# Splitting one more output product into quarters, a shared tile for its block sums, and fewer quarter products where v or o stands alone

## The chip, the cores and the metric

The kernel runs on one core of a Trainium2 chip. The metric is the device time of one execution in microseconds (us); the time of a kernel is the median over runs. TensorE (PE) multiplies, VectorE (DVE) and ScalarE (ACT) work on its results in PSUM, GpSimd (POOL) works in SBUF only, and SyncE (SP) issues the DMAs. PSUM has eight banks, and this kernel hands them out one by one.

## The reference, cut to what matters

Two layers on x of 64 x 256 x 512 (float32). Layer 0 is a graph layer; layer 1 is attention over 8 heads whose scores are masked by the adjacency matrix. All matrices are float32.

```python
h = relu(layernorm(x));  x = x + (adj @ h) @ W0 + b0          # layer 0
h = relu(layernorm(x))                                        # layer 1
q, k, v = h @ Wq + bq, h @ Wk + bk, h @ Wv + bv               # 512 x 512 each
attn = softmax(q k^T / 8 + (1 - adj) * -1e9)                  # 8 heads of 64
x = x + (attn v) @ Wo + bo
```

## The kernel before, in words

**Groups and stages.** The batch of 64 is worked on in 32 groups of two (`GB = 2`, `NG = 32`). Layer 0 runs over all groups first, then layer 1. In layer 1 the program is a software pipeline: for group g the loop at L1365 onwards issues `attend(g, 0)`, `score(g, 1)`, then q and k of group g+1 (the **QK stage**), `attend(g, 1)`, `score(g+1, 0)`, then v of group g+1 together with the output product o of group g (the **VO stage**). `qd` 0 and 1 are the first and second four heads. From group 2 on (`FIRST2`) the four projections q, k, v and o use a two-level scheme; groups 0 and 1 use the one-level `project`. So there are 30 two-level QK stages (groups 2 to 31), and 28 two-level VO stages (o of groups 2 to 29). v of group 2 is worked out beside a one-level o, v of group 31 alone (order `V1` in both), o of group 30 alone (order `O1`) and o of group 31 alone at the very end (order `OL`).

**Products.** Each projection is a Strassen-Winograd product: seven half-size products called A to G (table `BLOCKS`), on sums of weight halves (s1 to s4) and of activation halves (t1 to t4). A half-size product at **full form** is four matmuls of 128 rows with 256 columns (`product` inside `quartered`). If its letter is in `SMALL`, it is split once more: seven matmuls with 128 columns on sums of quarters (the **quarter form**). The quarter sums of weights are made once (`block_sums`, tiles named spare), those of the activations for every group on POOL (`block_hidden`, `block_outputs`, class `Blocks`). In `SMALL`, q, k and v have B to G, and o has C, D, E and F.

**Steps.** `quartered` makes a table of small steps, named by projection, letter and step: `qDg` is step g of product D of q. A step is one matmul, or one DVE add, or one ACT copy. Four ways of putting a quarter product together matter here. `added` (C, D, E): matmuls a, c, d, g into a fresh PSUM tile, and adds b, e, f, h from it into the SBUF result; h is a DVE add of 128 x 256 and the last reader of the tile. Matmuls i, j, k go into the bank of the product sum. `staged` (F, G): matmuls a, c, d, f; ACT copies b, e, g into an SBUF tile; DVE adds h and l. `chain` (B): matmuls a, d, b, f; ACT copies c, e, g, n; one DVE add k. `put` and `more` move a product sum into the result (steps such as `kp110`, `km10`).

**Order.** Nothing is scheduled by a tool: the engines run the steps in the order of the strings `QK`, `VO`, `V1`, `O1`, `OL` (L214 to L243), read by `follow`. A bar ends a tick, at which due work from `after` is issued (POOL's sums for instance), and an x issues one exponential of the scores on ACT. Every engine takes its own instructions in this order.

**Banks.** `bank()` hands out the first fitting entry of a list of free banks, and `give()` puts a bank at the end of the list when the last step that uses its tile has been issued. The program then waits, by a semaphore, until that last use is really over. A matmul that opens a tile in a bank just given back thus waits for the last DVE or ACT reader of the tile before it.

**Tiles.** q and k of the first four heads have one SBUF tile each per batch entry (tags q00, q01, k00, k01). The block sums of o live in a kept tile (`KEPT["o"]`), part of what layer 0 left free.

Of the kernel before, what the change touches and what calls it, by code (L numbers as in the profile page):

```python
# [73 lines left out]
def general_path(tc, x, adj, w0, b0, wq, bq, wk, bk, wv, bv, wo, bo, out):  # L74
# [140 lines left out]
    "qFa kA0 qFb kA1 kFa qFc x qCa | kA2 kA3 kFb qGa kp000 qFd kFc | kp001 kFd qA0 qFe kFe qA1 x qFf kFf | qA2 "  # L215
    "qFg kFg qA3 qFh kFi kFh qp000 kFj kFk qp001 | qCi kFl qCj x kCa qCk qCb qFi kCb qFj qCl qGb qCc kp100 qCd | "
    "qFl kCc kp101 kCd kGa x qCe qGc kCe qGd kCf kGi qCf kGj | qGe kGk kGb qFk kCg qp100 qGf kCh kGc qp101 qCg "
    "kGd | qGg qCh kBa kGe kBb qGh qGi kBc qGj kGf qGl qDa kGg kBd | qBa qDb kBe qBb kGh kBn qGk qBc qDc kGl qDd "
    "kBf qDe qBd | qDf kBg kCi kCj qBn kCk qBe kBh kCl kBi qDg qBf | qDh qEa qBg kEa kBj qEb kDa kEb kBk qBh qBi "
    "kDb qBj kp110 | kEc qBk kp111 qEc qEd kDc qp110 km11 kDd qp111 kDi kEd kDe qEf | kDj kDf kEf kDk qm11 kEi "  # L220
    "qEe kEj kEe qDi qEf2 kEk km10 kDg kEl0 | qEi kEf2 qDj kDh qDk qEg kEl1 qEj qm10 qEk kEg qEl0 | kEl2 kEh qEh "
    "qEl1 qEl2 ")
VO = (
    "vA0 oAz vA1 oBz vA2 vA3 x | vFa vCi vCj vCk vFb vp00 vBa vBb vFc x | vFd vGa vCl vFi vFj vFe vFk vBc vCa vGb "
    "vFf | vCb vBd vFg vGc vGd vBe vCc vFh vGe vCd vFl x oA0 oEa | vCe vGf vCf vBf vp10 oEb oA1 vGg vCg vBn oA2 "
    "vGh vBg | oA3 vCh x vGl oB0 vBh op00 oFa vBi | oFb vBj vDa vBk vEa vGi vDb vEb vGj vp11 vGk vEc | vDc vm11 "
    "vEd vDd vEe vDi vEf vDe vDj vDf vDk vEi vEf2 vEj | vm10 vEk vDg vEl0 vEg vDh oFc oFd vEl1 oFi vEh oFe oFj | "
    "vEl2 oFk oDa oFf oCa oFg oB1 oCb oB2 oFh | oFl oEc oEd oCc op10 oCd oB3 oCe oCi | oCf oCj op11 oG0 oG1 oDb "
    "oEe oG2 oEf | oG3 oDc om11 oDd oCg oDi oDe oDj oDf | oDk oEi oCh oCk om10 oDg oEj oEk oDh oEg oCl0 | oEh "
    "oCl1 oEl ")  # L230
V1 = (
    "vFa vA0 vFb vA1 vFc vDa x vFd | vA2 vA3 vFe vBa vp00 vBb vFf | vGa vBc vFg vFi vFj vGb vFh x vFk vGc vFl vBd "
    "vGd | vCa vBe vGe vCb vp10 vBf vGf vCc vBn vDb vBg vCd vGi vGg vCe vGj | x vCf vGk vEa vGh vBh vGl vBi vEb "
    "vBj x vDc vBk vDd | vEc vDe vEd vDf vCg vp11 vCi vCh vCj vEf vCk vEe vm11 vDg | vDi vDj vEf2 vDk vDh vEi vCl "
    "vEj vEg vm10 vEk | vEl0 vEl1 vEh vEl2 ")
O1 = (
    "oEa oAz oA0 oBz oA1 x oB0 | oFa oCa oEb oFb oA2 x oA3 oDa oFc | oFd oB1 oFe x oB2 oFf oEc oEd oFg op00 | oB3 "
    "oFh oFi oCb oFj op11 oFk oCc x oCd oFl | oCi oDi op10 oCj oDj oDk oDb oCk oEe oG0 oEf oCl0 oDc | oEg oG1 "
    "oCl1 oEh oDd oG2 oCe oCf oG3 oDe | oDf oCg om11 oDg oCh oEi oDh oEj oEk om10 | oEl ")
OL = (  # L240
    "oAz oBz oA0 oA1 oCa oA2 | oA3 oFa oB0 oFb oB1 | oB2 op00 oDa oFc oCb oFd oB3 oFe oFi op11 oFf | oFj oFg oFk "
    "oCi oCj oFh oDi oFl oDj oDk oEa op10 | oDb oEb oG0 om10 oDc oDd oCk oDe oEc | oDf oEd oG1 oCl0 oG2 oEe oG3 "
    "oEf oCl1 oDg om11 oEg | oCc oCd oDh oEi oCe oEj oCf oEk oEh oCg oEl | oCh ")  # L243
# [3 lines left out]
def kernel(  # L247
# [331 lines left out]
    SMALL = {"q": "BCDEFG", "k": "BCDEFG", "v": "BCDEFG", "o": "CDEF"}  # L579
# [3 lines left out]
    def block_sums(n):  # L583

        todo = []
        for x in SMALL[n]:
            w = W[n][BLOCKS[x][0]]
            def part(i, j):
                return w[:, j, i * P:(i + 1) * P]
            s1, s2, s4 = (spare.pop(0) for _ in range(3))  # L590
            W2[n, x] = dict(a11=part(0, 0), a12=part(0, 1), a22=part(1, 1), s1=s1, s2=s2, s3=part(1, 0), s4=s4)
            eng = nc.vector if x in "BFG" and n in "qk" else nc.gpsimd
            for o, p, q, op in ((s1, part(1, 0), part(1, 1), ALU.add), (s2, s1, part(0, 0), ALU.subtract),
                                (part(1, 0), part(0, 0), part(1, 0), ALU.subtract), (s4, part(0, 1), s2, ALU.subtract)):
                todo.append((eng.tensor_tensor, o, p, q, op))
        return todo

    class Blocks:

        def __init__(self, x, t):  # L600
            self.x, self.t = x, t
# [4 lines left out]
        def operand(self, n):  # L606
            if n == "t3":
                n = "b12"
            if n[0] == "t":
                return self.t[..., {"t1": 0, "t2": 1, "t4": 2}[n], :]  # L610
            return self.x[..., int(n[1]) - 1, int(n[2]) - 1, :]
# [5 lines left out]
    def quartered(g, n, halves, blocks, by_token, place, first, seeds=None, multiplied=None, done=None):  # L617

        s, steps, banks, users, adds, mms = W[n], {}, {}, {}, {}, [0]

        def step(name, todo, *used, quadrant=None, mm=False):
            mms[0] += mm
            for b in used:
                users[b] = users.get(b, 0) + 1
            if quadrant is not None:
                adds[quadrant] = adds.get(quadrant, 0) + 1

            def run_it():
                todo()
                for b in used:  # L630
                    users[b] -= 1
                    if not users[b]:
                        give(banks.pop(b), b in ("pa", "pc"))
                if quadrant is not None:
                    adds[quadrant] -= 1
                    if done and not adds[quadrant]:
                        done(*quadrant)
                if mm:
                    mms[0] -= 1
                    if multiplied and not mms[0]:  # L640
                        multiplied()
            steps[n + name] = run_it
# [26 lines left out]
        def product(x, b, fresh):  # L669
            if fresh and seeds:  # L670
                step(f"{x}z", lambda: take(b, seed=seeds[b][:, None, :].to_broadcast([P, 2, N])), b)
            for i in range(4):
                def todo(i=i):
                    starts = fresh and not seeds and i == 0
# [46 lines left out]
        def chain(x, b):  # L721
# [14 lines left out]
            def add_rest():  # L736
                o = part(banks[b], 1, None)
                add(o, o, like(o, held[0]))
            copy("c", 0, 0)
            step(x + "n", keep_rest, t)  # L740
            copy("e", 1, 0)
            copy("g", None, 1)
            last_three(x, "hij", b)
            step(x + "k", add_rest, b)
# [42 lines left out]
        if "B" in SMALL[n]:  # L787
# [4 lines left out]
        for x, name, end, i in (("F", "p10", put, 0), ("G", "m11", more, 1)):  # L792
            if x in SMALL[n]:
# [4 lines left out]
        added("C", lambda: place(0, 0), quadrant=(0, 0))  # L798
        last_three("C", "ijk", "pb", dict(partial=True))

        def add_three(name, m, k):
            def todo():
                o, u = (t if first is None else t.rearrange("p m (h j) -> p (m h) j", j=P)
                        for t in (place(0, 0), banks["pb"]))
                add(o[:, m, 0:k], u[:, m, 0:k], o[:, m, 0:k])
            step(name, todo, "pb", quadrant=(0, 0))
        for name, m, k in (("Cl0", 0, N), ("Cl1", 1, P)) if first is None else (("Cl", slice(0, 3), P),):
            add_three(name, m, k)
        added("D", lambda: place(1, 0), quadrant=(1, 0))
        last_three("D", "ijk", "pc")  # L810
# [263 lines left out]
    KEPT = {}  # L1074

    def block_hidden(g, step):
# [3 lines left out]
        third = Blocks(x[:, 1, 0:2, :].rearrange("p c (n j) -> p c n j", j=P), KEPT["h3"][:, 3])  # L1080
# [6 lines left out]

    def block_outputs(g, step):
        x = OT[g][:, 2:4, :].rearrange("p c (k n j) -> p k c n j", k=GB, j=P)
        t = KEPT["o" if g < NG - 1 else "h3"]  # L1090
        both = Blocks(x, t[:, 0:2])
        last = Blocks(HO[g].all[:, 1:3].rearrange("p t c (n j) -> p t c n j", j=P), t[:, 2:4])
        if g == NG - 1:
            for part in (last.one(0), last.one(1), both):
                part.sums(nc.gpsimd)
        elif g == NG - 2:
            after(step, last.sums, nc.gpsimd)
            behind_seeds.append(lambda: both.sums(nc.gpsimd))
        else:
            after(step, last.sums, nc.gpsimd)  # L1100
            after(step, both.sums, nc.gpsimd)
        O2[g] = {"C": both.one(0), "E": both.one(1), "F": last.one(0), "D": last.one(1)}

    def queries_keys(g):

        for n, store in (("q", Q), ("k", K)):
# [5 lines left out]
            def place(i, k, n=n, store=store):  # L1112
                if (i, k) not in store[g]:
# [47 lines left out]
    def quartered_outputs(g):  # L1161
        halves, place, done = outputs(g)
        row = L1["o"][1]
        return quartered(g, "o", halves, O2.pop(g), True, place, None, {"pa": row[:, :HF], "pc": row[:, HF:]}, done=done)
# [50 lines left out]
    def attend(g, qd):  # L1215
# [65 lines left out]

        after(1, divide)
# [82 lines left out]
    for g in range(NG):  # L1365
# [9 lines left out]
        if g == 0:  # L1375
            for pool, n, tag, used in ((const, 4 * DC, "w0_sb", None), (const, 4, "w0_s1", None), (const, 4, "w0_s2", None),
# [3 lines left out]
                                       (act, 16, "yT1", ("o", 4))):  # L1380
# [5 lines left out]
                spare.extend(t[:, i, :] for i in range(first, n))  # L1386
        for n, at in (("q", 7), ("k", 16)) if g == 0 else (("v", 9),) if g == 1 else (("o", 9),) if g == 2 else ():
# [15 lines left out]
        if g + 1 < NG:  # L1403
# [18 lines left out]
            else:  # L1422
                steps = quartered(g + 1, n, halves, H2[g + 1], *rest, multiplied=multiplied)
                if FIRST2 <= g < NG - 2:
# [59 lines left out]
```

## Time and profile before

| what | value |
|---|---|
| median of 3 runs | 2599.08 us (2598.89 to 2599.2) |
| profiled execution | 2598.82 us |
| its span in the profile | 2597.0 us |
| PE busy | 2580.3 us, 99% |
| weight loads (PEld) busy | 2299.8 us, 89% |
| DVE busy | 1903.8 us, 73% |
| ACT busy | 1254.3 us, 48% |
| POOL busy | 1792.4 us, 69% |
| layer 0 (all groups), q and k of group 0 | 0 to about 638 us |
| one group of layer 1 in the steady part (score, QK, attend, score, VO, attend) | 61.36 us |
| stage with v of group 31 alone | 11.57 us |
| stage with o of group 30 alone | 13.21 us |
| stage with o of group 31, first matmul to the start of the last | 14.59 us |

An engine's busy time is the union of its instructions' times. In a timeline each line gives start and duration in us, then engine, source line, operation and tiles. A float32 matmul stands in the trace as two rows (x2), and so does its weight load. Since matmuls are pipelined, the pace of a run of matmuls is read from start to start, not from the durations. "Idle before" is the time for which the engine had nothing to run, followed by what ended it. The granted clock of PE was full (0.999 on average).

### The profile page before, as it was taken

What the parts mean: (1) busy time and instruction counts of PE and PEld (TensorE: products, weight loads), DVE (VectorE), ACT (ScalarE), POOL (GpSimd) and SP (SyncE); (2) the same over time, 40 slices, a digit from 0 to 9 for tenths busy, and PEclk for the clock granted to TensorE, in tenths of its full rate; (3) what the DMA queues carried; (4) which work ended last, traced back from release to release, by engine and by line L of the source; (5) the groups of instructions that cost most, each with busy time, mean ns of one, the idle gap of its engine ahead of it and who ended that gap; (6) DMA issues with size and microseconds to landing.
All of it is one profiled execution on the core that took longest, in us unless ns stands there. A gap on an engine that the chain in (4) does not pass through costs nothing.

```text
span 2597.0 us, 56864 instructions
## 1 busy us (share of the span) xinstructions
PE 2580.3 (99%) x21914; PEld 2299.8 (89%) x21914; DVE 1903.8 (73%) x4160; ACT 1254.3 (48%) x2942; POOL 1792.4 (69%) x2150
## 2 busy tenths in 40 slices
PE   9999999999999999999999999999999999999998
PEld 8999899988888888888888888888888888888887
DVE  6888888885467677777777777777777777777776
ACT  4545444443344445555555455544445445554543
POOL 6788887773686666666666666666666666666665
PEclk9999999999999999999999999999999999999999
DMA  5676666565111222211111111111112222111101
GB/s 149 195 193 184 170 168 182 159 159 134 33 50 50 65 63 64 57 50 50 50 50 50 50 50 50 50 50 50 50 50 62 62 60 65 50 50 50 50 34 50
DMA packets 281107, 211.36 MB, mean 81 GB/s; under 512 B 145920, under 2 KB 212992, under 8 KB 280832
## 3 DMA queue, kind: packets, MB, share of 16 engines
q1 hardware_dynamic: 280224, 206.89, 30.0%
q8 instruction: 175, 2.87, 0.5%
q10 hardware_dynamic: 608, 0.79, 0.1%
q14 instruction: 100, 0.82, 0.1%
HBM read 106.96 MB, written 100.66 MB: 80 GB/s over the span
## 4 chain that ended last, share of the span: by engine, by line


## 5 line engine op out<-in xcount | busy, mean ns | idle before, releaser
L1188 DVE SCALAR_TENSOR_TENSOR a<-sc,maskT 128x512 f32<-128x512 f32 x512 | 311.9, 681 | 259.9 <-PE sc L1181 255.7
L1246 POOL TENSOR_TENSOR as<-as 128x512 f32<-128x512 f32 x64 | 80.8, 1263 | 411.0 <-ACT as L1245 404.9
L1213 POOL TENSOR_TENSOR as<-a 128x512 f32<-128x512 f32 x256 | 318.7, 1279 | 29.9 <-ACT a L1206 24.7
L1206 ACT ACTIVATE a<-a 128x1024 f32<-128x1024 f32 x256 | 272.6, 1065 | 3.6 <-DVE a L1188 3.6
L1181 PE MATMUL sc<-q,k 64*128 64x256 f32 x2048 | 238.7, 383 | 0.0
L1181 PEld LDWEIGHTS sc<-q,k 64*128 64x128 f32 x2048 | 194.5, 187 | 44.8 <-issue 26.3
L1229 PE MATMUL pav<-a,v 128*32 128x256 f32 x4096 | 232.7, 379 | 0.0
L1229 PEld LDWEIGHTS pav<-a,v 128*32 128x32 f32 x4096 | 132.9, 110 | 88.2
L43 DVE BATCH_NORM_STATS2 st<-x 128x6 f32<-128x512 f32 x256 | 173.1, 676 | 9.2 <-DMA x<-in_x_dram 6.8
L1236 ACT ACTIVATE as<-pden 128x512 f32<-128x512 f32 x64 | 38.3, 599 | 287.2 <-PE pden L1222 286.3
L1020 ACT ACTIVATE h<-x,nb,rs 128x512 f32<-128x512 f32 x128 | 97.2, 807 | 97.4 <-POOL nb L55 85.9
L516 POOL TENSOR_TENSOR oT<-oT 128x512 f32<-128x512 f32 x31 | 39.4, 1271 | 149.4 <-DVE oT L1267 149.4
L891 ACT ACTIVATE h<-x,nb,rs 128x512 f32<-128x512 f32 x124 | 90.8, 803 | 52.1 <-POOL nb L55 47.2
L703 ACT COPY q_F<-q_Fs 128x128 f32<-128x128 f32 (+1 forms) x90 | 27.1, 301 | 157.6 <-PE q_Fs L666 157.6
L1110 ACT ACTIVATE q<-q_pa,bq_c 128x256 f32<-128x256 f32 (+1 forms) x150 | 61.5, 451 | 62.0 <-PE q_pa L666 49.7
L954 POOL TENSOR_TENSOR hs<-h 128x512 f32<-128x512 f32 x31 | 39.5, 1273 | 72.9 <-ACT h L891 72.9
L1026 DVE STREAM_TRANSPOSE r<-h 128x512 f32<-128x512 f32 x128 | 83.9, 689 | 7.2 <-ACT h L1020 6.8
L615 POOL TENSOR_TENSOR spare<-h1T,spare 128x128 f32<-128x128 f32 x180 | 82.5, 459 | 7.1
L839 DVE TENSOR_TENSOR x<-o_pa,x 128x512 f32<-128x512 f32 (+1 forms) x121 | 82.4, 681 | 6.0 <-PE o_pa L680 4.9
L516 POOL TENSOR_TENSOR t_y<-yT,t_y 128x512 f32<-128x512 f32 (+1 forms) x65 | 82.7, 1272 | 2.9 <-ACT yT L926 0.5
L1248 POOL TENSOR_TENSOR as<-as 128x512 f32<-128x512 f32 x64 | 80.8, 1262 | 5.3
L516 POOL TENSOR_TENSOR t_h<-h1T,t_h 128x512 f32<-128x512 f32 x64 | 81.9, 1280 | 2.5
(1633 smaller groups left out, 8587.2 us busy)
## 6 DMA issues: line engine op xcount, KB each, us to landing
residual<-x SPq DMA_DIRECT2D x256, 128.0 KB, 2.5
hidden<-r SPq DMA_DIRECT2D x128, 256.0 KB, 4.4
h1T<-hidden SPq DMA_DIRECT2D x64, 512.0 KB, 7.3
x<-residual SPq DMA_DIRECT2D x32, 1024.0 KB, 8.2
x<-in_x_dram SPq DMA_DIRECT2D x254, 128.0 KB, 3.0
out_dram<-x SPq DMA_DIRECT2D x62, 512.0 KB, 4.2
w_sb<-in_L_gnn_weight_dram SPq DMA_DIRECT2D x1, 1024.0 KB, 8.9
wq_sb<-in_L_gnn_Wq_dram SPq DMA_DIRECT2D x1, 1024.0 KB, 6.8
```

Of the source, the lines that this page charges most:

```text
L43: nc.vector.bn_stats(st, src)
L516: eng.tensor_tensor(self.t[n][:, c, :], self.operand(p, c), self.operand(q, c), op=ALU.subtract)
L615: eng.tensor_tensor(self.operand(o), self.operand(p), self.operand(q), op=ALU.subtract)
L839: nc.vector.tensor_tensor(o, ps, u, op=ALU.add)
L891: nc.scalar.activation(H0[g][:, t, :], xt[:, t, :], AF.Relu, bias=nb[:, t % n:t % n + 1], scale=rs[:, t % n:t % n + 1])
L1020: nc.scalar.activation(h1[:, k * NT + t, :], xt[:, k * NT + t, :], AF.Relu, bias=nb[:, t:t + 1], scale=rs[:, t:t + 1])
L1026: nc.vector.transpose(r[:, :, k, t, :], h1[:, k * NT + t, :].rearrange("p (j b) -> p j b", b=32))
L1181: nc.tensor.matmul(ps[j][:, kt * N:(kt + 1) * N], k[j * HD:(j + 1) * HD, c, kt * P:(kt + 1) * P], q[j * HD:(j + 1) * HD, c, :], start=(kt ...
L1188: nc.vector.scalar_tensor_tensor(o.rearrange("p k n -> p (k n)"), ps[j], SCALE, maskT_f, op0=ALU.mult, op1=ALU.add)
L1206: nc.scalar.activation(a, a, AF.Exp)
L1213: nc.gpsimd.tensor_tensor(AS[c, b], a4[:, :, 0, :], a4[:, :, 1, :], op=ALU.add)
L1229: nc.tensor.matmul(po[f][h * 32:(h + 1) * 32, b * N:(b + 1) * N], v[:, k, h * HD + f * 32:h * HD + f * 32 + 32], A[h // 2, b][:, (h % 2) * ...
```

## The change

1. **o's G at quarter form.** `SMALL["o"]` gets G. `staged` then makes product G of o out of seven matmuls of 128 columns, three ACT copies and two DVE adds, in place of four matmuls of 256 columns. Its four activation sums (`head_outputs`) are made on POOL behind the score matmuls of the next group.
2. **One tile for q's and k's first head pairs and o's block sums.** The four tiles of tags q00, q01, k00, k01 become one tile of tag qk0; o's block sums take the same tag, in turn with it. The third sums (t3) of B, and of o's G, get a place of their own, so that the unsplit operand stays whole.
3. **Fewer quarter products where v or o stands alone.** v of group 2 and of group 31 has B at full form. o of groups 30 and 31 has only E and F at quarter form: C and D become four 256-column matmuls each (G was at full form there and stays).
4. **`chain` puts B together differently.** A copy of 128 x 128, one of 128 x 256 and one add of 128 x 256 go; one copy of 128 x 128 and two adds of 128 x 128 come.
5. **All five orders are new.** In the bank list pb is now given back as fully written where C is at full form.

```diff
-    SMALL = {"q": "BCDEFG", "k": "BCDEFG", "v": "BCDEFG", "o": "CDEF"}
+    SMALL = {"q": "BCDEFG", "k": "BCDEFG", "v": "BCDEFG", "o": "CDEFG"}
+    BOTH = {"v": "B", "o": "CDG"}
...
+            s3 = spare.pop(0) if x in BOTH.get(n, "") else part(1, 0)
+            W2[n, x] = dict(a11=part(0, 0), a12=part(0, 1), a22=part(1, 1), s1=s1, s2=s2, s3=s3, s4=s4)
...
-            def add_rest():
-                o = part(banks[b], 1, None)
-                add(o, o, like(o, held[0]))
+            def with_rest(name, k):
+                step(x + name, lambda: add(part(banks[b], 1, k), total(), held[0]), t, b)
             copy("c", 0, 0)
             step(x + "n", keep_rest, t)
-            copy("e", 1, 0)
-            copy("g", None, 1)
+            with_rest("e", 0)
+            copy("g", 0, 1)
+            with_rest("k", 1)
             last_three(x, "hij", b)
-            step(x + "k", add_rest, b)
...
+        if "C" in small:
+            added("C", lambda: place(0, 0), quadrant=(0, 0))
...
+        else:
+            product("C", "pb", True)
+            more("m00", "pb", 0, 0)
+        if "D" in small:
+            added("D", lambda: place(1, 0), quadrant=(1, 0))
+            last_three("D", "ijk", "pc")
+        else:
+            product("D", "pc", False)
...
+    def head_outputs(g):
+        O2["t"] = t = act.tile([P, 16, P], F32, tag="qk0", name=f"to_{g}")
+        head = Blocks(HO[g].all[:, 0].rearrange("p c (n j) -> p c n j", j=P), t[:, 12:15], t[:, 15])
+        head.sums(nc.gpsimd)
+        O2[g] = {"G": head}
...
-                if (i, k) not in store[g]:
+                if (i, k) not in store[g] and not i:
+                    if g not in QK0:
+                        QK0[g] = act.tile([P, 2, GB, 2, N], F32, tag="qk0", name=f"qk_{g}")
+                    store[g][i, k] = QK0[g][:, "qk".index(n), k]
...
+        if qd and FIRST2 <= g < NG - 2:
+            behind_scores.append(lambda: head_outputs(g))
         after(1, divide)
```

The part of the order `QK` around the handing over of a bank from D of q to D of k, before and after (PE steps are those ending in a, c, d, g of D and E; a, b, d, f, h, i, j of B; a, c, d, f, i, j, k of G):

```diff
-    ... kCl kBi qDg qBf | qDh qEa qBg kEa kBj qEb kDa kEb kBk qBh qBi kDb qBj kp110 | ...
+    ... | qDf kBj qBf kp110 qGc qBk qDg kp111 qGd qDh kDa qBg qEc qGe km11 | qEd qBh qEf qBi kDb ...
```

## The prediction

> **What bounds the kernel now.** I first read the page's busy shares, then the list of what PE waited for, then the busy time by stage, and last single timelines. The page's chain of waits is empty for this run, so the bound has to come from these.
>
> ```profile
> PE 2580.3 (99%) x21914; PEld 2299.8 (89%) x21914; DVE 1903.8 (73%) x4160; ACT 1254.3 (48%) x2942; POOL 1792.4 (69%) x2150
> ```
>
> ```profile
> PE w_27a L523 <- DVE x L839: 1.2, 1, 1.2
> ...
> PE o_pa L680 <- DVE x L839: 0.7, 1, 0.7
> ```
>
> ```profile
> 1464.35:1486.76 22.41, 22.41 (x186) 21.88 (x184) 17.52 (x43) 15.56 (x44) 11.88 (x18) 1.00 0.26 69
> ...
> 1494.87:1517.61 22.74, 22.74 (x175) 21.79 (x173) 18.98 (x45) 10.68 (x26) 18.39 (x19) 1.00 0.01 1
> ```
>
> The second block lists PE's waits (total, times, longest): all are one or two events each, in layer 0 or at the end, under 10 us in all. The third gives, for one QK and one VO stage, length, then busy time of PE, weight loads, DVE, ACT and POOL. PE fills both stages wholly, at full clock. So in 28 VO and 30 QK stages a matmul that goes is time that goes, and a wait put before a matmul is time that comes; no engine behind PE can give it back.
>
> **The pace of matmuls.** One VO stage runs product G of o at full form, then small matmuls:
>
> ```profile
> 1513.11 1.89 PE L680 MATMUL o_pa<-wo_s,t_o 128*128 128x256 f32 x8
> 1514.83 0.39 PE L666 MATMUL o_Ds<-spare,spare 128*128 128x128 f32 x2
> ...
> 1516.39 0.39 PE L666 MATMUL o_pb<-wo_sb,spare 128*128 128x128 f32 x2
> ```
>
> Four 256-column matmuls (x8) go from 1513.11 to 1514.83, 1.72 us; the next seven 128-column ones start from 1514.83 to 1516.17 and the eighth at 1516.39, so seven take 1.56 us, 0.223 each.
>
> **Part 1, G of o at quarter form.** Per VO stage 1.72 goes and 1.56 comes: -0.16 us, and x 28 = **-4.5 us**. The Trainium skill speaks against such a split: Perfetto Trace Analysis, section Matmuls, says that larger matmuls are more efficient when possible. The row agrees only in that a column costs 4% more (2 x 0.223 against 0.43); by a rule of no splitting I would book a loss, by the row seven small ones still beat four large ones. I take the row.
> What comes with it: three ACT copies (0.27, 0.27, 0.37 by the rows of v's G), two DVE adds (0.42 and 0.70 by v's), four POOL sums of 128 x 256 (0.73 each, 2.9 us). DVE goes from 18.98 to about 20.2 of 22.6 us, the change of `chain` for v included (two 0.28 for one 0.43); ACT and POOL stay below. PE hides all three as long as no matmul waits for a late one. DVE may end the stage later by the 1.25 us added: it then has nothing until the next scores (idle 4.00 before its mask operation at 1523.29), which covers it.
>
> **Part 2, the shared tile.** The new POOL sums must wait until the score matmuls have read q and k; these end at 1494.87. POOL is then idle until DVE's oT at 1498.60 (4.97 us idle), and the 2.9 us fit in with 0.8 left. Were that cover gone, o's other sums and the key sums would queue behind; the key sums end at about 1513.4, and PE wants them at 1517.61, so that 4 us of slip would still cost nothing. In the other direction, the first write of q and k into the tile comes in the next QK stage, and PE's last use of o's sums lies an attend and a score stage (4.45 and 3.65 us) earlier. Cost: nothing. The DMA queues get no instruction more or less; only in the last group one write of the result stands earlier on SP's queue, which is empty there. The extra weight sums (four on POOL, 0.46 each, once) lie in group 2's QK stage, where POOL works 11.9 of 22.4 us: nothing.
>
> **Part 3, v and o alone.** B of v at full form: +0.16 in each of two stages. But these stages have a stall that its chain causes:
>
> ```profile
> 762.64 0.39 PE L666 MATMUL v_Cs<-wv_sb,h1T 128*128 128x128 f32 x2
> 762.67 0.25 ACT L729 COPY v_pc<-v_Bs 128x128 f32<-128x128 f32 x1
> ...
> 762.97 0.30 PEld L666 LDWEIGHTS v_Bs<-spare,spare 128*128 128x128 f32 x2
> 762.97 0.49 PE L666 MATMUL v_Bs<-spare,spare 128*128 128x128 f32 x2
> 763.00 0.59 ACT L1124 COPY v<-v_pa 128x512 f32<-128x512 f32 x1
> ...
> 763.19 0.30 PEld L666 LDWEIGHTS v_Gs<-spare,spare 128*128 128x128 f32 x2
> ```
>
> The pair at 762.97 was due at 762.86 (0.22 after 762.64) and waits for the copy that ends at 762.92: 0.11 late, and its row is 0.49 rather than 0.39 long, 0.10 more, because its weights are loaded only after the wait. With two smaller ones beside it about 0.3 goes: net -0.14 each, **-0.3 us**.
> o alone: C and D cost 2 x 0.16 more in each of two stages, +0.64. These stages wait for DVE's answers: o of group 30 takes 13.21 us against a pace of 11.40 (28 small matmuls at 0.223, 12 large at 0.43), o of group 31 takes 14.59 to the start of its last matmul against 11.18. DVE works 11.58 us of the first. C and D at full form take about 2 us of adds out of each stage (by their rows two of 0.28 and two of 0.42 for each letter; C's sum of 0.70 gives way to one add of 0.69; neighbours overlap by 0.08). The pace after is 20 x 0.43 + 14 x 0.223 = 11.72, and 0.10 is lost at the entry of every stage. Bounds: all other stalls gone, -1.4 and -3.0; none gone, +0.3 each. With that much less on the engine they wait for I take most: -0.9 and -2.3, **-3.2 us**. The tail behind the last matmul keeps its form (adds of 128 x 256 from its bank, then the write): nothing.
>
> **Part 4, chain.** For q and k one ACT copy goes and a larger one shrinks; DVE swaps 0.43 for two 0.28. In QK DVE works 17.5 of 22.4 us: nothing.
>
> **Part 5, the new orders.** This decides. Each fresh PSUM tile takes a bank whose last reader must be done. I went through QK and VO in both programs' order, and counted the matmuls between the last one into the old tile and the first one into the new tile of the same bank. In the order before it is never under five matmuls (1.12 us), nor after, with one exception: D of k takes the bank of D of q, as before, but `kDa` now stands directly behind `qDh`, and only `qGd` lies between `qDg` and `kDa`. All other banks are in use there, so no other can be had, and in the built program that matmul does wait for DVE. How long the answer takes stands in the trace of before:
>
> ```profile
> 1479.97 0.39 PE L666 MATMUL q_Ds<-spare,spare 128*128 128x128 f32 x2
> ...
> 1480.39 0.42 DVE L839 TENSOR_TENSOR q<-q_Ds,q 128x256 f32<-128x256 f32 x1
> ...
> 1481.09 0.39 PE L666 MATMUL k_Ds<-t_h,wk_sb 128*128 128x128 f32 x2
> ```
>
> `qDg` starts at 1479.97, its add `qDh` 0.42 later and takes 0.42; release to matmul is 0.05 (762.92 to 762.97). Sum 0.89. Before, `kDa` came 1.12 after `qDg`, so 0.23 to spare. After, it is due 2 x 0.223 = 0.45 after it: 0.44 late. To this comes the restart. The Trainium skill (TensorE: Matmul & The Clock Gate, Step-by-step: what each phase is for) says that PE's queue pulls weight loads ahead of running matmuls; by that the weights would be in place and the stall 0.44, x 30 = 13.2 us. The rows at 762.97 show weight load and matmul starting together after the release, and the pair 0.10 longer; with it 0.54, x 30 = **+16.3 us**. I take the row. DVE is free then: the add before, `qBk`, starts 0.42 after its matmul `qBf` and ends at 0.70, while `qDg` comes two matmuls after `qBf` and its add is due at 0.87. Queued behind `kDa` on PE are the 29 last matmuls of the stage and all later stages; nothing on PE can pass it.
>
> **Sum** on the profiled execution: 2598.82 - 4.5 - 0.3 - 3.2 + 16.3 = **2607.1 us**; this execution lies 0.26 under the median of the runs, so I say 2607.3, +0.3%.
>
> **Rivals.**
> 1. *The bank wait does not show* (the answer comes in time, or another wait in QK already covers it). Then 2598.8 - 8.0 = 2590.8, -0.3%. For it: PE has not one wait in the QK stages now, and an order this regular elsewhere. Against: 0.89 against 0.45, from rows of the same three steps. 0.07.
> 2. *The stall is there without the restart*, or the o stages gain all: 2598.8 - 4.5 - 0.3 - 4.4 + 13.2 = 2602.8, within 0.2% of before. For it: the skill's rule. Against: each stalled pair above. 0.12.
> 3. *A second wait in QK.* The steps after `kDa` stand closer to their answers than before (`kDg` behind `kDf`, `kEg` behind the adds of E, `qDg` behind `qDf`), with DVE at 80%. One more wait of 0.05 with a restart of 0.10 in each of 30 stages is +4.5: 2611.6; two give 2616. For it: new, dense order; against: the wait at `kDa` itself gives DVE 0.5 us to catch up. 0.23.
> The forecast itself has 0.58.
>
> **How the numbers follow.** Cases of a slower kernel hold 0.81. What a measurement tells from no change is 0.2%, 5.2 us: from 2593.9 to 2604.3 counts as the same. The forecast's own spread is the o stages (+-1.5) and the stall (0.49 to 0.60, 14.7 to 18): 2604.5 to 2610, with a sliver below the bound. Slower 0.80, same 0.13, faster 0.07. For 8 in 10 the range takes in rival 2 in its upper half and one more wait of rival 3: 2602.5 to 2613.
>
> **What would show it.** Right: in each QK stage one wait of PE on a k_Ds matmul, ended by a DVE add from q_Ds, about 0.4 long with a pair of 0.49; QK stage 22.95 rather than 22.41, VO 22.58 rather than 22.74; the stage of o 30 near 12.3. Wrong: QK still at 22.4 (rival 1), QK at 22.85 (rival 2), waits in QK on other tiles (rival 3), or VO longer than 22.74, which would mean that DVE at 90% or POOL's late sums hold PE up.

## The result, and the profile after

The changed kernel takes **2615.94 us** (median of 6 runs, 2615.07 to 2616.59), the kernel before 2599.3 us beside it: 1.0064 times as long, 95% interval 1.0051 to 1.0077. That is +16.6 us where +8.2 was forecast, and above the forecast range, which ended at 2613. The profiled execution has a span of 2614.6 us against 2597.0.

The list of PE's waits, which had nothing in it from the QK stages, now begins with one (what waited, for whom, total us, times, longest):

```profile
PE k_Ds L671 <- DVE q L850: 8.8, 30, 0.3
```

Three stages of the changed kernel, a QK stage, the score stage ahead of a VO stage, and that of VO (columns as before: stretch, length, busy time of PE, weight loads, DVE, ACT, POOL, then granted clock, DMA share and GB/s):

```profile
1535.43:1558.55 23.12, 22.83 (x187) 22.03 (x185) 18.07 (x44) 15.62 (x42) 11.89 (x18) 1.00 0.24 65
1563.00:1566.77 3.77, 3.72 (x36) 3.03 (x32) 2.54 (x5) 0.60 (x1) 2.24 (x3) 1.00 0.02 4
1504.75:1527.32 22.57, 22.57 (x178) 21.83 (x179) 19.42 (x48) 11.13 (x27) 20.08 (x23) 1.00 0.00 1
```

QK was 22.41 and is 23.12, with a PE that is no longer busy throughout; VO was 22.74 and is 22.57; the score stage was 3.65 and is 3.77. Taken from the first matmul of a stage to the first of the next, over the whole execution:

| stages | before, each | after, each | difference in all |
|---|---|---|---|
| 30 QK | 22.41 | 23.13 | +21.6 |
| scores ahead of VO | 3.65 | 3.77 (28 of 33) | +3.4 |
| one score stage ahead of QK, longer before | 3.99 | 3.65 | -0.3 |
| 28 VO | 22.735 | 22.572 | -4.6 |
| v of group 2 beside a one-level o, and v of group 31 alone | 23.68, 11.56 | 23.55, 11.46 | -0.2 |
| o of 30, o of 31 | 13.21, 15.08 | 12.46, 13.15 | -2.7 |
| behind the last matmul | | | -0.8 |

Layer 0 is 1.1 us longer in this one execution (607.29 to 608.43), with the same instructions; it varies from run to run by this much (607.28 and 609.08 in two of the experiments) and is not the change's.

The wait that the forecast named, in one QK stage of the changed kernel (start, duration, engine, line, tiles; idle time before and who ended it):

```profile
2481.31 0.39 PE L671 MATMUL q_Ds<-spare,spare 128*128 128x128 f32 x2
2481.53 0.39 PE L671 MATMUL q_Gs<-t_h,wq_s 128*128 128x128 f32 x2
...
2481.74 0.42 DVE L850 TENSOR_TENSOR q<-q_Ds,q 128x256 f32<-128x256 f32 x1
...
2482.22 0.49 PE L671 MATMUL k_Ds<-t_h,wk_sb 128*128 128x128 f32 x2 [0.29 <-DVE q L850]
```

`kDa` was due at 2481.76 (0.45 after 2481.31) and comes at 2482.22, 0.06 behind the end of the add: 0.46 late. (The bracket says 0.29 because the row before it runs on until 2481.92.) Its pair of rows is 0.49 long and not 0.39, and the next one is that 0.10 later. In the mean over the stages 0.456 and 0.101, in sum 0.557; thirty times that is 16.7.

Later in the same stage stands a second wait, which the list of waits does not show, since a wait shorter than the overlap of the rows leaves no idle time:

```profile
2484.49 0.42 DVE L850 TENSOR_TENSOR q_G<-q_Gs,q_G 128x256 f32<-128x256 f32 x1 [0.34 <-ACT q_G L708]
...
2487.14 0.75 DVE L850 TENSOR_TENSOR k<-k_Ds,k 128x128 f32<-128x128 f32 x2
...
2487.68 0.39 PE L671 MATMUL q_pa<-spare,wq_s 128*128 128x128 f32 x2
2487.95 0.49 PE L671 MATMUL k_Ds<-spare,spare 128*128 128x128 f32 x2
```

The last line is `kDg`. It was due at 2487.90 and comes at 2487.95, and the row of 0.49 gives it away. It adds to rows of the tile that DVE must have read before (`kDe`, `kDf`, the two adds to 2487.89). Those adds end a row of DVE work, with pauses of 0.10 at most, that began with `q_G`, and `q_G` had waited for ACT. The wait and the longer row cost 0.15 in each stage, 4.5 in all.

The third is at the start of VO, here in the changed kernel:

```profile
1564.83 1.89 PE L1207 MATMUL sc<-qk 64*128 64x256 f32 x16
...
1566.15 0.60 ACT L309 ACTIVATE o_pa<-bo_r 128x512 f32<-128x512 f32 x1 [4.22 <-DVE a L1214]
1566.77 0.51 PEld L685 LDWEIGHTS v_pa<-wv_sb,h1T 128*128 128x128 f32 x3 [0.45 <-DVE a L1214]
1566.77 0.70 PE L685 MATMUL v_pa<-wv_sb,h1T 128*128 128x256 f32 x2
```

In the kernel before, the seed came behind the first matmul of VO, which started at 1494.87:

```profile
1494.97 0.60 ACT L309 ACTIVATE o_pa<-bo_r 128x512 f32<-128x512 f32 x1 [4.82 <-DVE a L1188]
```

VO now begins with `oAz vA0` where it began with `vA0 oAz`. ACT's seed for o thus gets the first bank that DVE's masking of the scores frees, and v's first matmul the next one, freed by a later mask operation: 0.12 us of PE, in 28 stages. (The second experiment below tests this.)

### The profile page after: what moved, and what is told of

The parts are those of the page before. It is cut to its first block, busy times and chain, and to the rows that moved or that the text cites. A ratio compares the mean times of both kernels' runs of the same rounds, so it can differ in the third digit from the quotient of the medians.

```text
span 2614.6 us, 57520 instructions
## 1 busy us (share of the span) xinstructions
PE 2589.6 (99%) x22046; PEld 2306.5 (88%) x22046; DVE 1957.1 (75%) x4284; ACT 1277.4 (49%) x2930; POOL 1837.0 (70%) x2262
## 4 chain that ended last, share of the span: by engine, by line
PE 87%; DVE 5%; POOL 3%; DMA 2%; issue 1%; ACT 1%; SPq 1%; DVEq 0%; POOLq 0%; ACTq 0%
PE pav L1255 8%; PE sc L1207 6%; DVE a L1214 3%; PE pden L1248 2%; PE q_pa L671 2%; PE k_pa L671 2%; PE v_pa L671 2%; PE v_pa L685 2%; PE o_pa L671 2%; PE o_pc L685 2%; PE o_pa L685 2%; PE q_pa L685 2%; PE k_pa L685 2%; PE q_pc L671 2%; PE k_pc L671 2%; PE k_Ds L671 2%
## 5 line engine op out<-in xcount | busy, mean ns | idle before, releaser
L1207 PE MATMUL sc<-qk 64*128 64x256 f32 x1024 | 119.2, 382 | 0.0
L1207 PE MATMUL sc<-q,k 64*128 64x256 f32 x1024 | 119.2, 382 | 0.0
L1207 PEld LDWEIGHTS sc<-q,k 64*128 64x128 f32 x1024 | 97.1, 187 | 22.4 <-issue 13.2
L1207 PEld LDWEIGHTS sc<-qk 64*128 64x128 f32 x1024 | 97.1, 187 | 22.3 <-issue 13.1
L708 ACT COPY k_F<-k_Fs 128x128 f32<-128x128 f32 (+1 forms) x90 | 27.2, 303 | 157.2 <-PE k_Fs L671 157.2
```

Of the source, the lines that this page charges most:

```text
L1207: nc.tensor.matmul(ps[j][:, kt * N:(kt + 1) * N], k[j * HD:(j + 1) * HD, c, kt * P:(kt + 1) * P], q[j * HD:(j + 1) * HD, c, :], start=(kt ...
```

## Experiments

A kernel called "three moves" below has all of the first three edits; the "fastest" is the one with `kEf2` earlier. Times are medians. The runs fall into batches on several chips, and the kernel before took 2598.4 to 2599.5 in them, so a difference between batches is uncertain by about 1 us; where that matters, the stages of the profiled executions are given as well. The last column is the mean of the 30 QK stages.

| what runs | expected | measured | QK stage |
|---|---|---|---|
| `kDa` later | 2599.2 | 2609.10 | 22.92 |
| VO begins with `vA0` | 2612.5 | 2613.17 | 23.12 |
| `kDg` later | 2611.5 | 2614.63 | 23.09 |
| three moves | 2591.3 | 2604.97 | 22.88 |
| three moves, DVE shifted by 3 | 2594.9 | 2594.22 | 22.544 |
| three moves, DVE shifted by 1 | 2594.2 | 2594.63 | 22.542 |
| `kDa` later, DVE shifted by 3 | 2599.0 | 2598.89 | 22.58 |
| three moves, `kEf2` earlier | 2591.2 | **2591.48** | 22.44 |
| before, `kDa` earlier | 2616 | 2601.47 | 22.52 |
| fastest, G of o at full size, shifted | 2596.0 | 2601.32 | 22.43 |
| fastest, G of o at full size | 2603 to 2606 | 2601.89 | 22.43 |
| fastest, part 3 undone for o | 2594.9 | 2594.87 | 22.44 |

### The three waits one by one

`kDa` alone moved:

```diff
-    ... kp111 qGd qDh kDa qBg qEc qGe km11 | qEd qBh qEf qBi kDb ...
+    ... kp111 qGd qDh qBg qEc qGe km11 | qEd qBh qEf kDa qBi kDb ...
```

> The changed kernel with one token of QK moved: kDa stands five matmuls behind qDg (about 1.1 us) instead of one. Theory (each wait is priced by itself: 0.456 late + 0.101 restart in each of 30 QK stages): -30 x 0.557 = -16.7, so about 2599.2 us, no wait on k_Ds behind q's add of D; the small wait at kDg (0.05 + 0.10) stays, since DVE is idle for 0.34 us ahead of the chain of adds that kDg waits for; QK stage about 22.56. Rival A: the order as a whole is too dense for DVE, and the wait at kDa only shows where it first catches PE; with it gone DVE has 0.56 us less to catch up in each stage and the wait reappears at kDg (up to 0.6 there): gain under 5, about 2611 to 2615, QK stage near 23.0. Rival B: the stall is not this wait: no change, 2616.

Measured 2609.10: only 6.8 of the 16.7 came. `kDa` waits no more, but `kDg` now waits for longer than it did, 0.39 (934.32 to 934.71 below) against 0.05:

```profile
PE k_Ds L671 <- DVE k L850: 6.8, 29, 0.3
```

By time and by QK stage this lies between the theory and rival A. But rival A had a busy DVE in mind, and DVE was not busy (same view as above, the kernel with `kDa` moved):

```profile
930.90 0.42 DVE L850 TENSOR_TENSOR q_G<-q_Gs,q_G 128x256 f32<-128x256 f32 x1 [0.58 <-ACT q_G L708]
931.36 0.70 DVE L850 TENSOR_TENSOR q_pa<-q_pa,q_G 128x512 f32<-128x512 f32 x1
932.52 0.69 DVE L850 TENSOR_TENSOR q<-q_pa,q 128x512 f32<-128x512 f32 x1 [0.46 <-ACT qk L1131]
933.12 0.68 DVE L850 TENSOR_TENSOR k<-k_pc,k 128x512 f32<-128x512 f32 x1
933.91 0.29 DVE L850 TENSOR_TENSOR k<-k_Ds,k 128x128 f32<-128x128 f32 x1
...
934.71 0.38 PE L671 MATMUL k_Ds<-spare,spare 128*128 128x128 f32 x1 [0.23 <-DVE k L850]
```

One separate wait stands between these adds: a semaphore wait that is an instruction of its own in DVE's stream (`EVENT_SEMAPHORE`). This line counts it and two later ones, and gives the start of the first and of the last:

```profile
L850 DVEq EVENT_SEMAPHORE  x3: 21/21/21, 932.1 to 936.0; - x3
```

Between 932.06, when the add to q_pa ends, and 932.52 DVE does nothing, though the wait is over at 932.1: 0.46, where 0.10 is usual at this place (2485.65 to 2485.75 in the changed kernel). The name in the bracket is inferred, and cannot be right. The add takes its q from an ACT operation that ended at 931.63, and not from the ACT write to qk. So neither theory explained the 0.35 us that are left beyond the usual. That became the open question.

```diff
-    "oAz vA0 vA1 oBz oA0 oA1 x | ...
+    "vA0 oAz vA1 oBz oA0 oA1 x | ...
```

> The changed kernel with the first two tokens of VO exchanged: v's first product takes the bank that the scores free first, o's seed the next one. Theory (v's first matmul now waits for a later mask operation of the scores, because o's seed took the first freed bank): the 28 score stages before VO go from 3.775 back to 3.654, -0.121 x 28 = -3.4, so about 2612.5 us. Rival: the entry of VO is late for something else (the later start of the scores' masks, or more work on ACT); then the stages stay at 3.775 and the time at 2616. A second rival: o's seed, now behind, holds up oA0, which is the fifth matmul of VO: then the score stage gets shorter and VO longer by as much, no gain.

Measured 2613.17, and all 33 score stages ahead of VO are back at 3.65 us, with VO unchanged at 22.572. The theory holds, both rivals fall.

```diff
-    ... | qEj qCl kEf qEk kDg kEf2 qEl0 qDi kEl2 qDj kDh qDk kEg ...
+    ... | qEj qCl kEf qEk kEf2 qEl0 qDi kDg kEl2 qDj kDh qDk kEg ...
```

> The changed kernel with kDg moved four matmuls later in QK. Theory (a wait of 0.048 at kDg with a restart of 0.101 in each of 30 stages): -30 x 0.149 = -4.5, so about 2611.5 us, and only the wait at kDa left in QK, of 0.46 as before. Rival A: the 0.149 goes to the next matmul that needs a late add (kEg or kDh's neighbours), no gain: 2616. Rival B: the restart of 0.101 is no cost by itself but only how a pair of rows is recorded; then moving a wait of 0.048 brings 1.4 us: 2614.5.

The edit moves `kDg` past one matmul (`qDi`), 0.22 us, and not past four as the expectation says; that is still more than the 0.05 of its wait. Measured 2614.63. This is rival B's number, but the trace has rival A: `kDg` comes on time, and the row of 0.49 now stands at `kEg`, three matmuls behind it (QK 23.08 in 28 of 30 stages, 0.04 less than in the changed kernel):

```profile
937.23 0.39 PE L671 MATMUL k_Ds<-spare,spare 128*128 128x128 f32 x2
...
937.90 0.49 PE L671 MATMUL k_Es<-spare,spare 128*128 128x128 f32 x2
```

The time alone would have told the wrong story.

All three moves together:

> All three moves together: kDa, the entry of VO, kDg. Theory (three separate waits, each priced from its rows): -16.7 - 3.4 - 4.5 = -24.6, so about 2591.3 us, below the kernel before by about 8.0, which is the sum of the parts 1 and 3 of the prediction (-4.5, -0.3, -3.2) with no wait left in QK. Rival: the waits share a cause (DVE too busy in the new order), so that the moves do not add up: 2597 to 2602.

Measured 2604.97. The gains of the three moves add up (6.8 + 2.8 + 1.3 = 10.9, measured 11.0), but 13.7 are missing. The key is in the stages: the first QK stage takes 22.54, the other 29 take 22.89 to 22.91. The same 0.35, and the same code in both.

### The stop in DVE's stream

What differs between the first QK stage and the others is where they stand in DVE's instruction stream. I counted DVE's instructions as the trace lists them, separate waits included. From one QK stage to the next there are 124 in the kernel before, 129 in the changed one, and 128 once `kDa` is moved, because one separate wait per stage goes (1047 in the whole trace of the changed kernel, 1017 then). With 128, the add that came late has number 1600, 1728, 1856 and so on: always 64 past a multiple of 128. In the first QK stage it has number 1490.

```diff
-    nc.vector.memset(mhalf, -0.5)
+    for _ in range(4):
+        nc.vector.memset(mhalf, -0.5)
```

> The kernel with the three moves (2605.0 us) and one thing more: a memset at DVE's start is issued four times instead of once, so that every later DVE instruction stands three places further on in DVE's stream. What it tests: in the runs with kDa moved, DVE stands still for 0.35 us ahead of one add (q from q_pa) in 29 of 30 QK stages, though its semaphores have long come; the two stages QK and VO then have exactly 128 DVE instructions, and that add is number 1600, 1728, 1856 and so on, each 64 more than a multiple of 128; in the first QK stage it is number 1490, and there is no such stop. Theory (DVE stops for about 0.35 us at each such place of its stream when it gets there without idle time): with the shift the place falls on the add of q_G, before which DVE waits 0.58 us for ACT anyway; the QK stages go from 22.89 to the 22.54 of the first one, 29 x 0.349 = 10.1, so about 2594.9 us. Rival (the stop has to do with the data or with PE's products that stand beside it, and so comes wherever kDa is moved): unchanged, 2605.

Measured 2594.22: three tiny instructions, issued once at the start, are worth 10.8 us by the medians (of two batches) and 10.1 by the QK stages. The same adds with the shift:

```profile
930.51 0.70 DVE L851 TENSOR_TENSOR q_pa<-q_pa,q_G 128x512 f32<-128x512 f32 x1
931.31 0.69 DVE L851 TENSOR_TENSOR q<-q_pa,q 128x512 f32<-128x512 f32 x1
931.92 0.68 DVE L851 TENSOR_TENSOR k<-k_pc,k 128x512 f32<-128x512 f32 x1
```

The pause from 931.21 to 931.31 is the usual 0.10, in all 30 stages. The rival, by which the stop has to do with the data or with the matmuls beside it, falls.

> The kernel with kDa alone moved (2609.1 us), and the same three places of shift in DVE's stream. Theory: kDa's wait is worth 30 x 0.557 = 16.7 as the prediction priced it, and 29 x 0.35 of it was lost to the stop in DVE's stream that the shift takes away: about 2599.0 us, QK stages at 22.58. Rival (DVE is too busy behind kDa, and the gain of kDa's move is lost at kDg whatever the place in the stream): 2609, QK stages at 22.93.

Measured 2598.89, no different from the kernel before (ratio 1.0001, interval 0.9991 to 1.0011). With the stop out of the way, moving `kDa` alone brings 17.0 us by the medians and 16.5 by the QK stages, 0.3 of which are two stops of the changed kernel (below): the prediction's price for this wait (16.3) was right. `kDg` waits on as in the changed kernel (it comes at 932.84, with a row of 0.49, 0.27 behind the matmul before it).

The rule did not hold as I had it. In the kernel with G of o at full size (below) the same stream number fell on the separate wait just ahead of the late add, and nothing stopped. In each stop that was seen the place was held by the instruction behind such a wait, single ones in the changed kernel (numbers 3520, 3904 and 4672) and in the kernel before (1856, 4032 and 5184) included. In all of these the instruction starts 0.40 to 0.42 after the wait's own record ends, where 0.04 is usual for the late add. Two of the single ones lengthen a QK stage of the changed kernel: the stages with 3520 and 4672 take 23.21 and 23.35, the other 28 take 23.11 to 23.12. Hence one more run, with a `range(2)` in the diff above:

> The kernel with the three moves (2605.0 us) and a shift of DVE's stream by one place instead of three. What it tests: in the run with G at full size and no shift, the place 64 past a multiple of 128 fell on the separate wait ahead of q's add from q_pa, and no stop was seen there; in each stop that was seen the place fell on the instruction just behind such a wait. Theory in its new form (DVE's front end needs about 0.35 us more for the instruction at that place; it runs ahead of the adds, so that this shows only if the instruction in front is a wait that has just been released, and is hidden behind a running add of 0.4 to 0.7 us otherwise): with the shift by one the wait itself stands at the place, behind the running add to q_pa of 0.70 us, and nothing is left of the stop: QK stages at 22.54, about 2594.2 us as with the shift by three. Rival (any add that DVE reaches without idle time is held up at that place): QK stages at 22.89, 2605.

Measured 2594.63. So the place must be held by an instruction that DVE reaches only when a wait has been released. That the delay otherwise lies hidden behind the 0.70 us add that is still running fits this run, but is not shown. Nor is the condition enough: in the kernel before, numbers 2368 and 4160 stand directly behind a released wait too, and start 0.02 and 0.12 after its record.

### The best version, and the other parts

`kEf` and `kEf2` earlier, against "three moves":

```diff
-    "kDe kEd kDf qCk kEe qEi kEl1 | qEj qCl kEf qEk kEf2 qEl0 qDi kDg kEl2 ...
+    "kDe kEd kDf qCk kEe kEf qEi kEf2 kEl1 | qEj qCl qEk qEl0 qDi kDg kEl2 ...
```

> The kernel with the three moves, and two tokens more moved in QK: kEf and kEf2 (DVE's add that kEg waits for) ahead of kEl1 and qCl, so that kEg's answer is there 0.75 us earlier. The DVE instructions of QK and VO together become 129 instead of 128, so that the stop in DVE's stream wanders from stage to stage, as in the changed kernel. Theory: no wait of PE is left in QK, stages at 22.41, no stop that repeats: 2615.9 - 30 x 0.71 - 28 x 0.121 = 2591.2 us. Rival: DVE's earlier kEf2 makes the adds kEl1 and qCl late for someone else, and a wait shows at the start of the attend stage or at kEl: 2594 to 2597.

Measured 2591.48, **faster than the kernel before**: ratio 0.9974, interval 0.9963 to 0.9984. The stages of this kernel (the same three kinds as above):

```profile
1523.80:1546.23 22.43, 22.43 (x186) 21.90 (x184) 17.88 (x44) 15.56 (x42) 12.02 (x18) 1.00 0.25 66
1550.69:1554.34 3.65, 3.65 (x36) 3.03 (x33) 2.42 (x5) 0.00 (x0) 2.23 (x3) 1.00 0.02 4
1493.12:1515.69 22.57, 22.57 (x180) 21.84 (x178) 19.53 (x48) 11.67 (x28) 19.95 (x23) 1.00 0.00 1
```

PE is busy for the whole of each again. The median is 6.9 under that of the kernel before beside it, the profiled execution 7.4. By stages, parts 1 and 3 give -8.1 (the prediction had -8.0), the one longer score stage of before gives -0.3, and the QK stages, 22.44 in the mean against 22.41, take 1.0 back.

The kernel before, with `kDa` alone at its new place:

```diff
-    ... | qDf kBg ... qDg qBf | qDh qEa qBg kEa kBj qEb kDa kEb kBk ...
+    ... | qDf kBg ... qDg qBf | qDh kDa qEa qBg kEa kBj qEb kEb kBk ...
```

> The kernel before with one token of QK moved: kDa directly behind qDh, as in the changed kernel, and all else of before. Theory: the place of kDa alone makes the wait of 0.456 and the restart of 0.101 in 30 stages: +16.7, about 2616 us, a wait of PE on k_Ds ended by DVE's add to q. Rival: before's order is looser, and kDa's bank comes in time, or the wait takes up slack elsewhere: 2599 to 2605.

Measured 2601.47, a miss. The premise was wrong: in the order of before another bank stands at the head of the list at that moment (that of B of k), so `kDa` gets it, and k's E takes the bank of D of q two matmuls later, 0.01 late, with a pair of 0.49: +0.11 per QK stage. `kDa` starts while the add from D of q has only begun:

```profile
1482.18 0.42 DVE L839 TENSOR_TENSOR q<-q_Ds,q 128x256 f32<-128x256 f32 x1
...
1482.20 0.39 PE L666 MATMUL k_Ds<-t_h,wk_sb 128*128 128x128 f32 x2
...
1482.66 0.49 PE L666 MATMUL k_Es<-h1T,wk_s 128*128 128x128 f32 x2
```

The place of `kDa` in the order makes no wait by itself; what counts is which bank heads the list of free ones at that place.

The fastest kernel with part 1 undone, and DVE shifted by 3:

```diff
-    SMALL = {..., "o": "CDEFG"}
+    SMALL = {..., "o": "CDEF"}
-    ... vDk | oFf vm10 vEi oFg vEj vEk oGa oFh vEl0 vCi oFl oGb vEg vCj | vCk vEl1 oGc vEl2 oGd vCl oCa oGe oFk ...
+    ... vDk | oFf vm10 vEi oFg vEj vEk oFh vEl0 vCi oFl vEg vCj | vCk vEl1 vEl2 vCl oCa oFk ...
```

(with `oGi`, `oGj`, `oGk` further on replaced by `oG0` to `oG3`)

> The fastest kernel so far (2591.5 us) with part 1 undone: o's G as four 256-column matmuls in VO again, without its copies and adds, and DVE's stream shifted by three places. Theory (7 small matmuls 1.56 us against 4 large 1.72): 28 x 0.163 = +4.6, so about 2596.0 us, VO stages at 22.735. Rival (G at quarter size gives a part back where PE waits for DVE's adds or ACT's copies, as larger matmuls would be the better form): no change or faster, 2589 to 2592.

Measured 2601.32, 5 us more than expected. VO takes 22.93 and not 22.735, for a reason of my order: without `oGc` and `oGd`, `oFk` comes too early for the add that it must follow (start of the add, then the matmul):

```profile
958.21 0.70 DVE L851 TENSOR_TENSOR o_pa<-o_pa,o_F 128x512 f32<-128x512 f32 x1
...
958.71 0.39 PE L672 MATMUL o_Cs<-wo_sb,oT 128*128 128x128 f32 x2
...
959.05 0.46 PE L672 MATMUL o_pa<-wo_s,to 128*128 128x128 f32 x2
```

`oFk` was due at 958.93 and comes at 959.05, 0.14 behind the end of the add, with a longer row: 0.20 in all. That and part 1's 0.163 make 28 x 0.36 = 10.1; measured are 9.8. The run agrees with the price of part 1 but does not measure it cleanly; the lengths of the VO stages (22.735 and 22.572) do.

The same without the shift:

> The same without the shift: QK and VO together then have 128 DVE instructions, and number 1600, 1728, 1856 and so on, where the theory has DVE stop for 0.35 us, is the wait just ahead of q's add from q_pa. Theory: 29 QK stages longer by 0.25 to 0.36 (what slack there is ahead of kDg and kEg is not known): 7 to 10 us above the kernel with the shift, 2603 to 2606. Rival (the stop belongs to the place of kDa or to the earlier order of QK): no more than 1 us apart.

Measured 2601.89, with QK stages as short as with the shift: the miss that led to the new form of the rule above.

Part 3 undone for o of groups 30 and 31: the orders `O1` and `OL` of before, with C and D in quarter products and their block sums.

```diff
-                         small="EF" if g >= NG - 2 else None)
+                         small="CDEF" if g >= NG - 2 else None)
```

> The fastest kernel so far (2591.5 us) with part 3 undone for o of the last two groups: C and D as quarter products and before's orders there. Theory (stages 0.74 and 1.93 shorter by part 3, and the end behind the last matmul by 0.8): +3.4, about 2594.9 us. Rival (the gain of these stages comes from a better order around them and not from fewer adds, or is taken back in the tail): 2591.5 to 2593.

Measured 2594.87. Part 3 is worth about 3 us for o: 3.4 by the medians of two batches, 2.7 when each is set against the kernel before beside it, and 0.75 and 1.93 by the two stages plus 0.3 at the end. The rival falls.

## Why the prediction was wrong

**The bound.** Right: PE's time by stage decides. The stage lengths of the profiled executions add up to +16.4, of +16.6 by the medians.

**Part 1** (-4.5): right, VO is 0.163 shorter, 4.6 in all. The rule that the prediction quotes from the Trainium skill (Perfetto Trace Analysis, Matmuls), that larger matmuls are more efficient when possible, holds for a column and not for the product: seven matmuls of 128 columns stream 896 columns, four of 256 stream 1024, and the seven were faster.

**Part 2** (0): nothing of it shows in a stage; it was not tried alone. **Part 4** (0): no wait was traced to it, and it too was not tried alone.

**Part 3** (-0.3 and -3.2): -0.2 and -3.4. The sum is right by some luck: the two o stages gave 0.74 and 1.93 (forecast 0.9 and 2.3), and the end behind the last matmul, costed at nothing, gave 0.8 in these two executions. Over all runs that end takes 5.6 to 6.1 with the new form and 6.3 to 6.6 with the old, so its share is not exact.

**Part 5** (+16.3). The wait at `kDa` was right in place, cause and size: 0.456 and 0.101 against 0.44 and 0.10, and 16 to 17 us when it was taken away. The restart, for which I took the trace's row over the rule of the Trainium skill (TensorE: Matmul & The Clock Gate, Step-by-step: what each phase is for) that weight loads are pulled ahead of running matmuls, was seen at each wait between small matmuls, 0.07 to 0.10.

**What failed** is the step "I went through QK and VO in both programs' order, and counted the matmuls between the last one into the old tile and the first one into the new tile of the same bank". It found "one exception", and there were three. The count looked at one kind of dependency only. It passed over matmuls that add to a tile which DVE must first read (`kDg`, 4.5 us), and over banks that do not come from a matmul's tile in the same stage but from DVE's masking of the scores (start of VO, 3.4 us, less the 0.3 of the one longer score stage). 8.2 forecast + 0.4 at `kDa` + 4.5 + 3.1 = 16.2, of 16.6; 0.3 more are the two single stops of DVE in QK.

The first of them stood in the text as **rival 3**, with its exact size (0.05 + 0.10) and `kDg` by name, at 0.23. I set against it that "the wait at `kDa` itself gives DVE 0.5 us to catch up". That was the wrong argument: the row of DVE work ahead of `kDg` starts with an add that waits for ACT's copy of a PE result behind `kDa`, so a pause of PE moves both alike. The run with `kDa` moved and DVE shifted shows it: without the wait at `kDa`, `kDg` is as late as with it. The wait at the start of VO stood nowhere in the text.

## What to carry to other kernels

When an order is rewritten, list every matmul that waits for another engine, the ones that add to a tile already read included, and every buffer that comes from the stage before; one kind of dependency counted carefully is not a count. A wait of PE can hide from a list of idle times: look for rows longer than their neighbours. Where equal stages of one kernel differ by a constant, compare where they stand in an engine's instruction stream before a new cause is sought in the data.

## What was not expected of the hardware

DVE stood still for about 0.35 us at certain places of its instruction stream, with all that it waited for done. It was seen only when the instruction at the place stands directly behind a separate wait that has just been released, and not at every such place (2368 and 4160 in the kernel before). All stops of this kind that were found in layer 1, in the kernel before, the changed one and the experiments, are at stream numbers 64 past a multiple of 128. With 128 instructions per pair of stages the stop came back in 29 of 30 stages, 10 us in all; with 124 or 129 it wanders and costs little (0.3 us in the QK stages of the changed kernel). A change that adds or takes away one wait per pair of stages can thus move this kernel by 0.4%. The Trainium skill (Runtime: NRT & Kernel Launch, Instruction fetch mechanics) says that instructions are fetched in blocks, of 256, and that the cost of going from one to the next is mostly hidden. The runs have a period of 128 and not of 256, and a cost that was not hidden where it mattered. That it is fetching is not shown; that the place in the stream matters is.

The matmul pairs (128 columns, two rows) that were seen to wait for a semaphore took 0.46 to 0.49 where the others take 0.39, even where the wait was 0.01 us: at `kEg`, `kDg` and k's E the fixed 0.10 was most of the price.
